# How many maxima scores each group takes, by weights of two engines' work, and the order of heads in the exp scores

## The chip, the cores and the metric

The kernel runs on one core of one Trainium2 chip. The metric is the device time of one execution in microseconds; the times shown are medians of a few executions.

## The reference, cut to what matters

The input has 8 batches of 1024 tokens of width 256. A block of attention with 16 query heads and 4 key heads of width 16, and then a linear layer with weights of -1, 0 and 1, each between two layer norms and with a residual:

```python
h = layernorm(x)                                  # over the 256 columns
q, k, v = h @ Wq, h @ Wk, h @ Wv                  # 256, 64, 64 columns
q, k = rope(q), rope(k)                           # q over all 256 columns, k per head
scores = einsum('bhqd,bhkd->bhqk', q, k) / 16     # 16 heads, keys repeated 4 times
o = softmax(scores) @ v
x = x + layernorm(o @ Wo)
f = layernorm(x) @ (ternary(W) * alpha).T + bias
x = x + layernorm(f)
```

All is float32. The softmax subtracts the largest score of its row, so the largest score must be known before the exponentials are taken.

## The kernel before, in words

**Units, blocks, steps, scores.** A unit is half a batch, 512 queries; there are 16 units (`NU`). A unit has 4 blocks (`G`), a block 8 key tiles (`NK`), so there are 512 steps of one key tile each (`NSTEP`), and a step has four matmuls of exp scores. The index `s` counts exp scores, from 0 to 2047; 128 of them make a unit, 32 a block.

**Two passes over the scores.** Each score is made twice on TensorE. `max_scores(v)` (line 582) makes 128 queries by 512 keys in one half of a PSUM tile `sm` of two banks; VectorE reduces the tile to row maxima `mx` (line 607), in one instruction of 1024 elements, or in two of 512 where `reduce_early` takes the first half at the end of a group. There are 2048 such scores too, two to a tile, and two `sm` buffers. When a block's maxima are complete, `shift_join`, `shift_rows` (a transpose `pm`, line 630) and `shift_low` (`ml`, on VectorE) split the maxima into a high and a low part, and a DMA writes them into spare rows of the queries `q_st`, so that the second matmul subtracts them by itself. `exp_one(s)` (line 655 for the matmul `se`, line 671 for the exponential `e` on ScalarE) makes 128 keys by 512 queries of one head group. Its tiles `se` come from a pool of three PSUM banks, which the other stages share: every transpose and product (`pt_xt`, `pt_ot`, `pq`, `pkv`, `pa`, `pf`, `pm`) takes one of the three. `e` has 12 buffers.

**Row halves.** The four heads of a step are two in rows 0 to 63 of the array and two in rows 64 to 127 (`a` is 0 or 1). Maxima scores have a half as well: from the second block on, two maxima of one tile are on one half, and the next tile's on the other. In PE's queue an exp score and a maxima score follow each other, and the two can be in the array together if their halves differ.

**Groups.** `window(s)` issues a group: `window_size(s)` exp scores, two or three, interleaved with maxima scores; then stages of other work that are ready (`do_parts`); then the products with the values, `av_piece` (line 691), of the group two groups back. From score 40 on (`REGULAR`) a group has two exp scores when a stage that needs a PSUM bank is ready, and that one stage; else three exp scores and none. The tensor engine's order is written by hand in this way (`tc.manual_schedule`), VectorE's and ScalarE's too; GpSimd's is left to the scheduler in the middle part.

**How far the maxima are ahead.** `maxima_by(s)` is the number of maxima scores that must have been issued when exp score `s` is: `s + 40`, and 2 more at six points, so `s + 52` from score 100 on. Before, a group takes as many maxima as bring the count to it: apart from the six points as many as it has exp scores. The last 13 steps have no maxima left, and `exp_two` makes their scores in `sm` tiles.

**Other stages.** `todo` maps a step to stages: `P_PARTS` for the projections of a later unit (`begin` is a layer norm's statistics on VectorE, `x` transposes, `kv_and_dram`, `q`, `v`), `T_PARTS` for what follows attention in the unit before (`invert` is a reciprocal on VectorE, `attn` the product with `Wo`, `stats_a`, `stats_x`, `stats_f` are statistics on VectorE, `ffn` the linear layer). The pattern recurs every 128 exp scores.

Of the kernel before, what the change touches and what calls it, by code (L numbers as in the profile page):

```python
# [28 lines left out]
def kernel(  # L29
# [35 lines left out]
    NK = S // P  # L65
# [4 lines left out]
    NSTEP = NU * SPU  # L70
    LEAD, START = 13, 10
# [121 lines left out]
    ffn = {}  # L193
# [361 lines left out]
    def block_queries(i, r2=slice(None)):  # L555

        u, j = divmod(i, G)
        if u < NU - 1:
            return q_st[u % 2][:, j, r2, :]
        return q_st[u % 2][:, :, r2, j * P : (j + 1) * P]  # L560

    def head_and_tile(i, r2, t):
        return r2 * UT + t if i // G < NU - 1 else 2 * t + r2

    def max_scores(v):


        i, k = divmod(v // 2, 2 * NK)
        u, part = i // G, v % 2
        if i == 0:  # L570
            a, ch, t, r2 = 1 - part, k // NK, k // 2 % UT, k % 2
        else:
            a, ch, t, r2 = 1 - k % 2, part, k // 4, k // 2 % 2
        queries = block_queries(i, r2)
        queries = queries[:, t * P : (t + 1) * P] if u < NU - 1 else queries[:, t]
        if part == 0:
            sm[0] = ps_mx.tile([P, 2, 512], F32, tag="sm", name=f"sm_{i}_{k}")
            if k == 0:
                mx[i] = small.tile([P, 2, 2 * UT, 2], F32, tag="mx", name=f"mx_{i}")
            reduced.clear()  # L580
        rows = slice(64 * a, 64 * a + 64)
        scores = nc.tensor.matmul(  # L582
            sm[0][:, part, :],
            queries[rows],
            k_st[(u // UPB) % 3][rows, r2, ch * 512 : (ch + 1) * 512],
            start=True,
            stop=True,
        )
        if part == 0:
            return  # L590
        if reduced:
            tc.declare_no_dep(scores.ins, early[0], reason="another bank")
        if i == 0:
            nc.vector.tensor_reduce(
                mx[i][:, ::-1, head_and_tile(i, r2, t), ch], sm[0], AX.X, ALU.max
            )
        else:
            reduce_halves(i, k, 2)
        if k == 2 * NK - 1:
            shift_join(i)  # L600
            due.append((v // 4 + (1 if i < 3 else 2), i))

    def reduce_halves(i, k, n):

        lo = len(reduced)
        a, t, r2 = 1 - k % 2, k // 4, k // 2 % 2
        early[0] = nc.vector.tensor_reduce(  # L607
            mx[i][:, a, head_and_tile(i, r2, t), lo:n], sm[0][:, lo:n, :], AX.X, ALU.max
        ).ins
        reduced.extend(range(lo, n))  # L610

    def reduce_early(v):

        i, k = divmod(v // 2, 2 * NK)
        if i > 0 and v % 2:
            reduce_halves(i, k, 1)
# [3 lines left out]
    def shift_join(i):  # L620

        m = mhl[i] = small.tile([P, 2, 2, 2 * UT], F32, tag="mc", name=f"mc_{i}")
        halves = mx.pop(i).unsqueeze(2).to_broadcast([P, 2, 2, 2 * UT, 2])
        nc.vector.tensor_reduce(m, halves, AX.X, ALU.max)
# [26 lines left out]
    def exp_scores(n, r2, a, sc):  # L651
        i, kt = divmod(n, NK)
        queries = block_queries(i, r2)
        rows = slice(64 * a, 64 * a + 64)
        nc.tensor.matmul(  # L655
            sc if len(queries.shape) == 2 else sc.rearrange("p (j t) -> p j t", j=G),
            k_st[(i // G // UPB) % 3][rows, r2, kt * P : (kt + 1) * P],
            queries[rows],
            start=True,
            stop=True,  # L660
        )

    def exp_one(s):

        n, (a, r2) = s // 4, divmod(s % 4, 2)
        assert n // NK in shifts
        i, kt = divmod(n, NK)
        e = es[n, r2, a] = ep.tile([P, UQ], F32, tag="e", name=f"e_{i}_{kt}_{r2}_{a}")
        sc = ps_e.tile([P, 512], F32, tag="se", name=f"se_{i}_{kt}_{r2}_{a}")
        exp_scores(n, r2, a, sc)  # L670
        nc.scalar.activation(e, sc, AF.Exp, scale=1.0 / D**0.5)  # L671

    def exp_two(n, r2):

        i, kt = divmod(n, NK)
        sc = ps_mx.tile([P, 2, 512], F32, tag="sm", name=f"se_{i}_{kt}_{r2}")
        for a in range(2):
            exp_scores(n, r2, a, sc[:, a, :])
        for a in range(2):
            e = es[n, r2, a] = ep.tile([P, UQ], F32, tag="e", name=f"e_{i}_{kt}_{r2}_{a}")  # L680
            nc.scalar.activation(e, sc[:, a, :], AF.Exp, scale=1.0 / D**0.5)

    def av_piece(i, first, end):

        va = v_aug[(i // G // UPB) % 3]
        if first == 0:
            av_ps[0] = ps_av.tile([P, UQ], F32, tag="av", name=f"av_{i}")
        for kt in range(first // UQ, (end - 1) // UQ + 1):
            lo, hi = max(first - kt * UQ, 0), min(end - kt * UQ, UQ)
            for r in (1, 2, 3, 0):  # L690
                nc.tensor.matmul(  # L691
                    av_ps[0][32 * r : 32 * r + 32, lo:hi],
                    va[:, kt, r, :],
                    es[i * NK + kt, r // 2, r % 2][:, lo:hi],
                    start=(kt == 0 and lo == 0),
                    stop=(kt == NK - 1 and hi == UQ),
                )
# [341 lines left out]
    def maxima_by(s):  # L1039

        return s + 4 * START + 2 * sum(s >= k for k in (28, 36, 52, 68, 84, 100))

    def banked(f, args):

        return f in (shift_rows, threshold, transpose_ternary) or (
            f is part and args[2] in ("x", "q", "v", "kv_and_dram", "attn", "ffn", "n", "o")
        )

    REGULAR = 40
    ends = 4 * (NSTEP - LEAD)  # L1050


    ready = []

    def window_size(s):


        left = 4 * NK - s % (4 * NK)
        if s >= ends:
            return 4  # L1060
        if s == 6:
            return 2
        size = min(2 if s >= REGULAR and any(banked(*p) for p in ready) else 3, left, ends - s)
        if left - size == 1:
            size += 1 if size == 2 else -1
        return size

    maxima = [0]

    def collect(n):  # L1070

        if due and due[0][0] <= maxima_by(4 * n + 4) // 4 - 1:
            i = due.pop(0)[1]
            ready.insert(0, (shift_rows, (i,)))
        ready.extend(todo.pop(n, ()))

    def do_parts(banks):

        while ready:
            f, args = ready[0]  # L1080
            if banked(f, args):
                if banks == 0:
                    break
                banks -= 1
            ready.pop(0)
            f(*args)
            if f is shift_rows:
                split_later.append(args[0])

    def take_low():  # L1090
        while split_later:
            shift_low(split_later.pop(0))

    def start_step(n):
        for q in range(4):
            max_scores(maxima[0])
            maxima[0] += 1
            if q == 1:
                take_low()
        collect(n)  # L1100
        do_parts(99)
# [3 lines left out]
    def av_windows(lag):  # L1105

        while len(behind) > lag:
            i, s, size = behind.pop(0)
            first = s % (4 * NK)
            av_piece(i, first * P, (first + size) * P)  # L1110
            if first + size == 4 * NK:
                done.append(i)

    def window(s):


        late, size = s >= ends, window_size(s)
        if done:
            av_out(done.pop())
        if late:  # L1120
            for r2 in range(2):
                exp_two(s // 4, r2)
        else:
            end = min(maxima_by(s + size), 4 * NSTEP)
            for q in range(max(size, end - maxima[0])):
                if q < size:
                    exp_one(s + q)
                if maxima[0] < end:
                    max_scores(maxima[0])
                    maxima[0] += 1  # L1130
                if q == 0:
                    take_low()
            reduce_early(maxima[0])
        take_low()
        behind.append((s // (4 * NK), s, size))
        for n in range(s // 4, (s + size) // 4):
            collect(n)
        do_parts(3 - size if REGULAR <= s < ends else 99)
        av_windows(1 if late else 2)
        return s + size  # L1140

    E = mybir.EngineType
    due, picks = [], []
    with tc.manual_schedule(engines={E.PE, E.DVE, E.Activation, E.Pool}):
# [52 lines left out]
        s = 0  # L1197
        while s < 8:
            s = window(s)
    with tc.manual_schedule(engines={E.PE, E.DVE, E.Activation}):  # L1200
        while s < 4 * NSTEP:
            s = window(s)
# [73 lines left out]
```

## Time and profile before

| | us |
|---|---|
| median of 3 runs | 1642.32 (1642.08 to 1643.09) |
| the profiled execution | 1642.63 |
| its span, first to last instruction | 1640.8 |
| PE, DVE, ACT, POOL busy | 1579.7, 1399.3, 1274.8, 835.4 |
| first exp score at | 62.7 |
| one unit of 128 exp scores, in the middle | about 96.4 |

The first 62.7 us are the start; from there to about 1620 us the pattern of groups runs; the rest is the last unit's tail. PE is TensorE's matmuls, PEld its weight loads (each matmul has one), DVE is VectorE and ACT is ScalarE. [...] Ends of matmuls are modelled.

### The profile page before, as it was taken

What the parts mean: (1) busy time and instruction counts of PE and PEld (TensorE: products, weight loads), DVE (VectorE), ACT (ScalarE), POOL (GpSimd) and SP (SyncE); (2) the same over time, 40 slices, a digit from 0 to 9 for tenths busy, and PEclk for the clock granted to TensorE, in tenths of its full rate; (3) what the DMA queues carried; (4) which work ended last, traced back from release to release, by engine and by line L of the source; (5) the groups of instructions that cost most, each with busy time, mean ns of one, the idle gap of its engine ahead of it and who ended that gap; (6) DMA issues with size and microseconds to landing.
All of it is one profiled execution on the core that took longest, in us unless ns stands there. A gap on an engine that the chain in (4) does not pass through costs nothing.

```text
span 1640.8 us, 37250 instructions
## 1 busy us (share of the span) xinstructions
PE 1579.7 (96%) x14712; PEld 818.5 (50%) x14712; DVE 1399.3 (85%) x2049; ACT 1274.8 (78%) x2479; POOL 835.4 (51%) x1239
## 2 busy tenths in 40 slices
PE   7999999999999999999999999999999999999997
PEld 5544455454545545454544545455454544444544
DVE  7778788889898888989889898988989888898964
ACT  4657778878787887878788787887878787877884
POOL 5532457374653737455373835547374552323363
PEclk8989999999999999999999999999999999999999
DMA  4151425125151422515133251513325151231100
GB/s 139 53 101 34 91 77 101 59 76 101 56 106 49 91 67 82 101 46 105 60 83 75 77 106 44 104 49 89 71 67 104 40 97 42 46 70 34 42 15 27
DMA packets 86079, 117.99 MB, mean 72 GB/s; under 512 B 12088, under 2 KB 50808, under 8 KB 85752
## 3 DMA queue, kind: packets, MB, share of 16 engines
q1 hardware_dynamic: 85904, 115.60, 29.9%
q8 instruction: 116, 1.90, 0.5%
q14 instruction: 59, 0.48, 0.1%
HBM read 68.65 MB, written 45.88 MB: 70 GB/s over the span
## 4 chain that ended last, share of the span: by engine, by line
PE 80%; DVE 10%; DMA 3%; ACT 2%; POOL 2%; issue 2%; SPq 1%; POOLq 0%; DVEq 0%; ACTq 0%
PE av L691 28%; PE se L655 28%; PE sm L582 9%; DVE mx L607 7%; PE pa L283 3%; PE pq L283 2%; PE pf L283 2%; PE pt_ot L267 2%; ACT e L671 2%; PE pt_xt L267 2%; PE pkv L283 2%; DMA q_st<-ml 1%; DMA k_rot<-d_k 1%; PE pm L630 1%; DMA dk<-ks 1%
## 5 line engine op out<-in xcount | busy, mean ns | idle before, releaser
L607 DVE TENSOR_REDUCE mx<-sm 128x2 f32<-128x1024 f32 (+1 forms) x1304 | 1205.3, 973 | 191.9 <-PE sm L582 174.1
L671 ACT ACTIVATE e<-se 128x512 f32<-128x512 f32 x1996 | 1058.2, 602 | 223.0 <-PE sm L582 172.4
L582 PE MATMUL sm<-k_st,q_st 64*128 64x512 f32 x2048 | 748.4, 450 | 6.9 <-DVE mx L607 3.9
L655 PE MATMUL se<-q_st,k_st 64*128 64x512 f32 x2048 | 705.5, 441 | 26.7 <-ACT e L671 14.4
L691 PE MATMUL av<-e,v_aug 128*32 128x256 f32 (+3 forms) x8608 | 607.2, 378 | 0.0
L655 PEld LDWEIGHTS se<-q_st,k_st 64*128 64x128 f32 x2048 | 324.9, 185 | 405.7 <-ACT e L671 302.1
L582 PEld LDWEIGHTS sm<-k_st,q_st 64*128 64x128 f32 x2048 | 326.1, 185 | 65.1 <-DVE mx L607 41.9
L691 PEld LDWEIGHTS av<-e,v_aug 128*32 128x32 f32 x8608 | 194.4, 108 | 211.0 <-issue 148.3
L241 POOL TENSOR_SCALAR lnsc<-mv 128x2 f32<-128x2 f32 (+1 forms) x134 | 25.8, 193 | 400.1 <-DVE mv L239 395.1
L765 POOL TENSOR_TENSOR xn<-xn,a 128x512 f32<-128x512 f32 x30 | 38.4, 1282 | 131.8 <-DMA a<-d_rec 101.2
L826 POOL TENSOR_TENSOR a<-a,bias_bc 128x512 f32<-128x512 f32 x30 | 38.6, 1287 | 108.3 <-ACT a L825 108.3
L242 POOL TENSOR_TENSOR lnsc<-lnsc,mhalf 128x2 f32<-128x2 f32 (+1 forms) x134 | 92.5, 691 | 0.9
L162 POOL TENSOR_TENSOR hl<-xn,hl 128x512 fp32r<-128x512 f32 x60 | 76.5, 1287 | 0.4
L253 POOL TENSOR_SCALAR xn<-x,lnsc 128x256 f32<-128x256 f32 x116 | 65.1, 570 | 2.2
L237 DVE BATCH_NORM_STATS2 bnst<-a 128x6 f32<-128x256 f32 x120 | 44.5, 413 | 4.6 <-POOL a L826 4.6
L297 POOL TENSOR_TENSOR t<-q_rot,sin_q_sb 128x512 f32<-128x512 f32 x31 | 39.9, 1288 | 15.5 <-ACT q_rot L439 15.4
L283 PE MATMUL pa<-woh,hl 128*128 128x256 f32 x240 | 46.2, 294 | 1.1 <-ACT e L671 1.1
L283 PE MATMUL pq<-xt,wqkvh 128*128 128x256 f32 x256 | 45.8, 303 | 0.5 <-ACT e L671 0.5
L237 DVE BATCH_NORM_STATS2 bnst<-x 128x6 f32<-128x256 f32 x124 | 45.9, 412 | 0.4 <-DMA x<-in_L_attn_x 0.4
L271 ACT CAST ot<-pt_ot 128x512 fp32r<-128x512 f32 x66 | 39.6, 601 | 4.7 <-PE pt_ot L267 4.7
L439 ACT COPY q_rot<-pq 128x512 f32<-128x512 f32 x32 | 18.8, 586 | 30.9 <-PE pq L283 30.9
L162 POOL TENSOR_TENSOR hlq<-q_rot,hlq 128x512 fp32r<-128x512 f32 x31 | 39.8, 1285 | 4.8 <-ACT hlq L159 4.5
(157 smaller groups left out, 1303.1 us busy)
## 6 DMA issues: line engine op xcount, KB each, us to landing
q_st<-dq SPq DMA_DIRECT2D x90, 256.0 KB
dq<-hlq SPq DMA_DIRECT2D x60, 256.0 KB
d_av<-avsb SPq DMA_DIRECT2D x60, 256.0 KB
x<-in_L_attn_x SPq DMA_DIRECT2D x15, 512.0 KB
xn<-d_av SPq DMA_DIRECT2D x30, 256.0 KB
a<-d_rec SPq DMA_DIRECT2D x30, 256.0 KB
xr<-in_L_attn_x SPq DMA_DIRECT2D x15, 512.0 KB
out_x<-a SPq DMA_DIRECT2D x30, 256.0 KB
```

The costliest lines, as they stand in the source:

```text
L162: eng.tensor_tensor(lo, src, hi.bitcast(F32), ALU.subtract)
L237: nc.vector.bn_stats(st[:, t, :], src[:, t, :])
L242: nc.gpsimd.tensor_tensor(sc[:, 1, :], sc[:, 1, :], mhalf[:, :n], ALU.pow)
L253: eng.tensor_scalar(dst[:, t, :], src[:, t, :], sc[:, 0, t : t + 1] if eng is nc.gpsimd else mv[:, t, 0:1], sc[:, 1, t : t + 1], ALU.add i ...
L267: nc.tensor.transpose(pt[:, c, t * P : (t + 1) * P], src[:, t, c * P : (c + 1) * P], ident_r)
L283: nc.tensor.matmul(out, chunk(left[i], c), chunk(right[j], c), start=(k == 0), stop=(k == len(steps) - 1),)
L297: eng.tensor_tensor(dst, x, table.unsqueeze(1).to_broadcast(list(x.shape)), ALU.mult)
L582: scores = nc.tensor.matmul(sm[0][:, part, :], queries[rows], k_st[(u // UPB) % 3][rows, r2, ch * 512 : (ch + 1) * 512], start=True, stop= ...
L607: early[0] = nc.vector.tensor_reduce(mx[i][:, a, head_and_tile(i, r2, t), lo:n], sm[0][:, lo:n, :], AX.X, ALU.max).ins
L655: nc.tensor.matmul(sc if len(queries.shape) == 2 else sc.rearrange("p (j t) -> p j t", j=G), k_st[(i // G // UPB) % 3][rows, r2, kt * P : ...
L671: nc.scalar.activation(e, sc, AF.Exp, scale=1.0 / D**0.5)
L691: nc.tensor.matmul(av_ps[0][32 * r : 32 * r + 32, lo:hi], va[:, kt, r, :], es[i * NK + kt, r // 2, r % 2][:, lo:hi], start=(kt == 0 and lo ...
```

## The change

A group no longer takes a fixed number of maxima. `maxima_of(s, size)` keeps an account `behind_by` of how far VectorE's work is behind TensorE's, in units of about 10 ns. For each possible number `n` (1, 3 or 5 in a group of three; 2 or 4 in a group of two; never below what `maxima_by` asks, and never over 12 ahead of it) it reckons the tensor engine's time and VectorE's, and takes the largest `n` that leaves the account under 60. Stages enter with weights of their own (`W_PE`, `W_DVE`). Below score 40 the number is what it was.

`pairs(size, n)` writes the order in the group: two maxima of different halves may follow each other, and an exp score ahead of a maxima score is taken from the other half. So the exp scores of a block no longer come in the order of `s`: `waiting` has a list for each half, and `exp_next(a)` takes the next of one. A block's shift falls due by the number of maxima issued (5 or 9 after its last), and it is asked for in every group rather than at whole steps. The end of the maxima is found by counting (`ended`) rather than fixed at 13 steps.

```diff
-            due.append((v // 4 + (1 if i < 3 else 2), i))
+            due.append((v + (5 if i < 3 else 9), i))
...
-    def exp_one(s):
-        n, (a, r2) = s // 4, divmod(s % 4, 2)
+    waiting = [[], []]
+    def exp_next(a):
+        n, r2 = waiting[a].pop(0)
...
     REGULAR = 40
-    ends = 4 * (NSTEP - LEAD)
+    AHEAD = 12
...
+    def ended(s):
+        return maxima[0] == 4 * NSTEP and s % 4 == 0 and len(waiting[0]) == len(waiting[1])
...
+    W_SCORES, W_PAIR, W_AV, W_AV_COLS, W_MAX = 19, 23, 14, 21, 58
+    W_PE = {"q": 162, "attn": 162, "kv_and_dram": 162, "ffn": 113, "v": 33}
+    W_DVE = {"begin": 92, "stats_a": 92, "stats_x": 92, "stats_f": 92, "invert": 46}
+    place = [0]
+    behind_by = [60]
+    def part_weight(table, f, args, default):
+        return table.get(args[2], default) if f is part else default
+    def maxima_of(s, size):
+        least = min(maxima_by(s + size), 4 * NSTEP) - maxima[0]
+        if s < REGULAR or maxima[0] == 4 * NSTEP:
+            return max(least, 0)
+        other = [part_weight(W_PE, *p, 44) for p in ready if banked(*p)][: 3 - size]
+        best = None
+        for n in range(2 - size % 2, 6, 2):
+            if n < least or maxima[0] + n > min(maxima_by(s + size) + AHEAD, 4 * NSTEP):
+                continue
+            time = W_SCORES + W_PAIR * (n + size) // 2 + W_AV + W_AV_COLS * size + sum(other)
+            rest = behind_by[0] + W_MAX * n - time
+            if best is None or rest < SLACK:
+                best = n
+        return max(least, 0) if best is None else best
+    SLACK = 60
+    def sm_half(v):
+        i, k = divmod(v // 2, 2 * NK)
+        return 1 - v % 2 if i == 0 else 1 - k % 2
+    def pairs(size, n):
+        first = maxima[0]
+        halves = [sm_half(first + k) for k in range(n)]
+        left = [len(w) for w in waiting]
+        def exp_on(a):
+            a = a if left[a] else 1 - a
+            left[a] -= 1
+            return a
+        order, k = [], 0
+        while k < n:
+            if size < n - k and k + 1 < n and halves[k] != halves[k + 1]:
+                order += ["max", "max"]
+                k += 2
+            elif size:
+                order += [exp_on(1 - halves[k]), "max"]
+                size -= 1
+                k += 1
+            else:
+                order.append("max")
+                k += 1
+        for _ in range(size):
+            order.append(exp_on(0 if left[0] >= left[1] else 1))
+        return order
...
     def do_parts(banks):
+        if due and due[0][0] <= max(maxima[0], maxima_by(place[0])):
+            ready.insert(0, (shift_rows, (due.pop(0)[1],)))
         while ready:
             f, args = ready[0]
             if banked(f, args):
                 if banks == 0:
                     break
                 banks -= 1
+                behind_by[0] -= part_weight(W_PE, f, args, 44)
+            behind_by[0] += part_weight(W_DVE, f, args, 0)
...
     def window(s):
...
-            end = min(maxima_by(s + size), 4 * NSTEP)
-            for q in range(max(size, end - maxima[0])):
-                if q < size:
-                    exp_one(s + q)
-                if maxima[0] < end:
+            n = maxima_of(s, size)
+            order = pairs(size, n)
+            behind_by[0] += W_MAX * n - W_SCORES - W_PAIR * len(order) // 2
+            for q, what in enumerate(order):
+                if what == "max":
                     max_scores(maxima[0])
                     maxima[0] += 1
-                if q == 0:
+                else:
+                    exp_next(what)
+                if q == 1:
                     take_low()
...
+        behind_by[0] = max(0, behind_by[0] - W_AV - W_AV_COLS * size)
```

More of the change, by code (lines that the diff above doesn't have):

```diff
@@ L1049 @@
     REGULAR = 40
-    ends = 4 * (NSTEP - LEAD)
+    AHEAD = 12
     ready = []
+    def ended(s):
+        return maxima[0] == 4 * NSTEP and s % 4 == 0 and len(waiting[0]) == len(waiting[1])
     def window_size(s):
         left = 4 * NK - s % (4 * NK)
-        if s >= ends:
-            return 4
         if s == 6:
             return 2
-        size = min(2 if s >= REGULAR and any(banked(*p) for p in ready) else 3, left, ends - s)
+        size = min(2 if s >= REGULAR and any(banked(*p) for p in ready) else 3, left)
+        if maxima[0] == 4 * NSTEP:
+            size = min(size, 4 - s % 4)
         if left - size == 1:
@@ L1068 @@
     maxima = [0]
     def collect(n):
-        if due and due[0][0] <= maxima_by(4 * n + 4) // 4 - 1:
-            i = due.pop(0)[1]
-            ready.insert(0, (shift_rows, (i,)))
         ready.extend(todo.pop(n, ()))
     def do_parts(banks):
+        if due and due[0][0] <= max(maxima[0], maxima_by(place[0])):
+            ready.insert(0, (shift_rows, (due.pop(0)[1],)))
         while ready:
@@ L1114, in window @@
     def window(s):
-        late, size = s >= ends, window_size(s)
+        late = ended(s)
+        place[0] = s
+        size = 4 if late else window_size(s)
+        if s % (4 * NK) == 0:
+            for n in range(s // 4, s // 4 + NK):
+                for a in range(2):
+                    waiting[a] += [(n, r2) for r2 in range(2)]
         if done:
@@ L1122, in window @@
                 exp_two(s // 4, r2)
-        else:
-            end = min(maxima_by(s + size), 4 * NSTEP)
-            for q in range(max(size, end - maxima[0])):
-                if q < size:
-                    exp_one(s + q)
-                if maxima[0] < end:
+            for w in waiting:
+                del w[:2]
+        else:
+            n = maxima_of(s, size)
[3 more added lines that the diff above has]
+                if what == "max":
                     max_scores(maxima[0])
                     maxima[0] += 1
-                if q == 0:
+                else:
+                    exp_next(what)
+                if q == 1:
                     take_low()
@@ L1137, in window @@
             collect(n)
-        do_parts(3 - size if REGULAR <= s < ends else 99)
+        do_parts(3 - size if s >= REGULAR and not late else 99)
         av_windows(1 if late else 2)
+        behind_by[0] = max(0, behind_by[0] - W_AV - W_AV_COLS * size)
         return s + size
```

## The prediction

> **What bounds the kernel now.** I read the page's chain first, then the waits, then VectorE by form, then one unit of 128 exp scores as stretches and in order of time.
>
> ```profile
> PE 80%; DVE 10%; DMA 3%; ACT 2%; POOL 2%; issue 2%; SPq 1%; POOLq 0%; DVEq 0%; ACTq 0%
> ```
> The tensor engine's queue carries the chain; VectorE has a tenth of it, 0.10 x 1640.8 = 164 us. The waits, as engine and line, releaser, total us, times, longest:
>
> ```profile
> PEld se L655 <- ACT e L671: 302.1, 651, 0.9
> DVE mx L607 <- PE sm L582: 174.1, 274, 3.4
> PEld sm L582 <- DVE mx L607: 41.9, 127, 1.4
> ```
> These are weight loads; the long first row is partly covered by matmuls still running. The third row is what VectorE's lateness leaves idle at the loads, the second what VectorE waits for scores: it is late in some groups and idle in others. By form (busy us, mean ns):
>
> ```profile
> L607 DVE TENSOR_REDUCE mx<-sm 128x2 f32<-128x1024 f32 x712 | 855.3, 1216 | 167.5 <-PE sm L582 153.2 <-PE se L655 11.0
> L607 DVE TENSOR_REDUCE mx<-sm 128x1 f32<-128x512 f32 x592 | 381.9, 680 | 24.5 <-PE sm L582 20.9
> ```
> In the timeline the starts of two in a row are 1.13 us apart for the first form (803.00 and 804.13) and 0.60 for the second. A group of three takes one of each, 1.73 us; the fastest group of three takes 1.46 us from first exp score to next (838.38 to 839.85). So VectorE falls behind in runs of such groups and catches up where a product stands in the group. One unit, in three stretches (length; PE, PEld, DVE, ACT, POOL busy):
>
> ```profile
> 774.94:788.00 13.06, 12.61 (x124) 5.55 (x120) 12.95 (x20) 10.69 (x22) 4.90 (x8) 1.00 0.34 110
> 788.00:806.24 18.24, 18.22 (x177) 9.87 (x173) 15.08 (x20) 14.30 (x28) 5.38 (x6) 1.00 0.03 9
> 806.24:855.81 49.57, 48.29 (x467) 25.84 (x463) 41.89 (x62) 39.00 (x76) 34.99 (x52) 1.00 0.27 76
> ```
> VectorE is full in the first (12.95 of 13.06), has 3.2 us left in the second and 7.7 in the third. Why it is full: a layer norm's statistics and a reciprocal among the maxima.
>
> ```profile
> 775.38 0.74 DVE L237 BATCH_NORM_STATS2 bnst<-x 128x6 f32<-128x256 f32 x2
> 776.03 0.30 DVE L239 BATCH_NORM_AGGREGATE mv<-bnst 128x2 f32<-128x6 f32 x2
> 776.26 0.33 DVE L639 SCALAR_TENSOR_TENSOR ml<-mh,low,pm 32x128 fp32r<-32x128 f32 x1
> ...
> 781.12 0.53 DVE L752 RECIPROCAL den<-den 128x64 f32<-128x64 f32 x1
> ```
> What it costs the tensor engine: in a pair both loads should start together, and here the third is split.
>
> ```profile
> 780.56 0.19 PEld L655 LDWEIGHTS se<-q_st,k_st 64*128 64x128 f32 x1
> 780.57 0.19 PEld L582 LDWEIGHTS sm<-k_st,q_st 64*128 64x128 f32 x1
> 780.80 0.18 PEld L655 LDWEIGHTS se<-q_st,k_st 64*128 64x128 f32 x1
> 781.24 0.18 PEld L582 LDWEIGHTS sm<-k_st,q_st 64*128 64x128 f32 x1 [0.26 <-DVE mx L607]
> ```
> The products behind it wait too: this group lasts 780.46 to 782.46, 2.00 us.
>
> **What the Trainium skill says.** "TensorEngine Tiling (Array Packing)", Key Properties: different tiles of the array load weights and multiply in parallel. The trace agrees: loads of opposite halves start within 0.01 us (780.56, 780.57). Where the halves are equal, as at 118.68 to 120.37, the four matmuls start at 118.68, 119.02, 119.25 and 119.49, so a score alone takes about 0.23 us. "TensorE: Matmul & The Clock Gate", Part 3, The mechanism: matmuls keep their order, start and end; so a late maxima score holds all behind it, as above. "VectorE: DVE Perf Modes", The perf-mode tier table: `tensor_reduce` has only the 1x mode; no faster form is behind 1216 and 680 ns. "Perfetto Trace Analysis", Identifying the Most-Contended Engine: matmul occupancy is no measure of headroom; 96% here goes with the waits listed.
>
> **The change, part by part.** From the built order: 793 groups in both. 64 groups of three exp scores take one maxima score instead of three, and 66 groups of two with a stage take four instead of two; about 380 of some 450 plain groups of three stay as they are. Reductions: 728 full and 592 half before, 712 and 624 after: 32 x 0.60 - 16 x 1.13 = +1 us of VectorE. In the middle the pattern recurs per unit: four of the first kind and four of the second.
>
> *(a) Relief.* Two of the four light groups stand at scores 920 and 928, right behind the statistics and the reciprocal, in the first stretch. They take 2 x 1.13 = 2.26 us of maxima out of it. The splits between an exp load and its maxima load there (0.33 at 777.45, 0.44 at 780.80, 0.21 at 782.57, 0.48 at 784.62, 0.23 at 786.42, 0.28 at 788.48) sum to 2.0 us; I take 1.9 off the path. What is late next is the exponential: three take 1.46 us at their 0.485 us spacing, so the light group doesn't go below that.
>
> *(b) Where they go.* The other two light groups (947 and 957) and the four heavy ones (945, 950, 952, 960) lie in the second stretch: net four maxima more, 2.3 us of reductions in 3.2 us of room. On PE a heavy group has a third slot: 4 x 0.23 = +0.92. A light group saves a slot only if its two last exp scores differ in half; in the built order 33 of 64 have equal halves, so about 2 x 0.23 = -0.46. The four maxima need both `sm` tiles within some 0.3 us, and the stage's product stands behind them in PE's queue, as do its evacuation and the next exp scores: I add 0.35 for tiles not yet free. Sum +0.8.
>
> *(c) Shifts.* `pm` at 918 shares a group with `begin`, and the group after it takes 2.40 us (774.94 to 777.34) instead of 1.68. After the change the shift comes 13 exp scores earlier and apart from it. Of four shifts per unit, two had a group of three behind them, after it one: -0.3. The two DMAs of a shift (8 KB each) and those of `stack_queries` keep their order on SP; the maxima of a unit start up to 12 scores, 12 x 0.75 = 9 us, earlier, which leaves 60 scores, 45 us, from the issue of its queries' load at score 128(u-1)+4, so I cost that at nothing; without this cover it would be a wait of its landing at each unit. `xr` and the projections' loads don't move.
>
> *(d) The order of heads.* Exp scores of a half may now run ahead, so the products with the values meet a younger `e`: in four groups per unit the youngest `e` that a first product needs has only one exp score behind it, against three groups in the whole kernel before. No wait of that size is in the trace (PEld av on ACT e is 5.1 us in 21). Bounds: nothing, where the stage between covers it; 0.7 us each at most (exponential of the second score of a group ends 1.6 us after its start, the products begin at 0.9). I take 0.1 each, +0.4, keeping 0 to 2.8.
>
> Per unit -1.9 + 0.8 - 0.3 + 0.4 = -1.0 us, in ten units (3 to 12): -10. In units 13 to 15 the loads' idle time for VectorE is larger (5.0 us in 1339 to 1432 against 1.6 in the unit shown), and there are about five light groups each, most behind statistics: -2.5 + 1.2 + 0.3 = -1 each, -3. Between scores 40 and 100 the count ahead was not a multiple of four for about 48 scores, so exp and maxima scores were of equal halves; they now differ: 24 pairs or so x 0.23 = 5.5, part under other waits, -4. The start (62.7 us) and the tail keep their work; the maxima end up to 12 scores sooner, which frees VectorE where nothing waits for it: 0. Sum -17 against the profiled execution (1642.63, 1.8 more than its span and 0.3 over the median): 1626 us.
>
> **The rivals.** *More than that:* all of VectorE's share of the chain is in play; if a third of its 164 us goes, 1590 to 1608. For it: it idles 174 us waiting for scores. Against it: the 302 us of waits for exponentials, unchanged, and most groups keep their number. 0.12. *No effect:* the wait for VectorE turns into one for the exponential; (a) falls to 0.6 and the sum to between -8 and +3. For it: 1.46 us of exponentials in a group of 1.68. 0.20. *Slower, by the order of heads:* the products in av wait for a young `e`, at 4 places per unit; at 0.35 us each a unit's sum is nought, from 0.5 each on the whole is over 0.2% slower, and at 0.7 a unit loses 1.4 us: 13 units +18, less 4: 1646 to 1657. For it: PE keeps its order, so the wait is paid in full. Against it: the next exp scores wait for ScalarE anyhow. 0.16. *That it does not do what it says* is excluded for the order, which shows the numbers above; what is open is whether weights in steps of 10 ns follow the true backlog. The forecast has 0.52.
>
> **How the numbers follow.** A measurement of this kernel can tell about 0.2%, 3.3 us. Faster: 0.52 + 0.12 + half of the no-effect case, 0.10 = 0.74; same 0.09; slower 0.16 + 0.01 = 0.17. The forecast's own range is 1615 to 1634, from (d) at 0, (a) at 2.0 and (b) without its 0.35 (-5, -1, -5) up to (d) at 0.2 each and no gain in units 13 to 15 (+5, +3). For 8 in 10 it reaches to 1604 and 1647, into both outer cases.
>
> **What would show it.** Right: 0.3 us or less between the loads of a pair behind `begin` and `invert`; PEld sm waiting for DVE mx under 30 us; DVE's share of the chain down to 5 to 7%; a middle unit in about 95.4 us. (d) shows as a row of av waiting for e, over 20 us if the slow rival holds. Wrong: units of 96 us or more, or a gain that lies before score 100 alone.

## The result, and the profile after

The changed kernel takes 1667.2 us (1666.98 to 1668.79); the kernel before took 1642.24 beside it. The ratio is 1.0153, 95% interval 1.0135 to 1.0171: 25 us slower where 16 us faster was forecast. The profiled execution took 1666.98 us with a span of 1665.2, against 1642.63 and 1640.8.

The page's chain and the row of the tensor engine, of the changed kernel:

```profile
PE 1607.2 (97%) x14736; PEld 829.9 (50%) x14736; DVE 1402.9 (84%) x2065; ACT 1275.0 (77%) x2479; POOL 834.9 (50%) x1239
...
PE 75%; DVE 13%; DMA 5%; POOL 4%; ACT 2%; issue 2%; SPq 1%; POOLq 0%; ACTq 0%
```
VectorE's share of the chain rose from 10 to 13% where it was to fall, and PE's busy time grew by 27.5 us with the same number of score matmuls. The waits of the changed kernel:

```profile
PEld se L655 <- ACT e L673: 244.4, 588, 0.9
DVE mx L607 <- PE sm L582: 179.5, 273, 5.7
...
ACT e L673 <- PE se L655: 63.3, 113, 4.9
PEld sm L582 <- DVE mx L607: 53.8, 125, 1.2
...
PEld av L693 <- ACT e L673: 12.8, 58, 0.4
```
The wait of a maxima score for VectorE, which the change was to shorten, grew from 41.9 to 53.8 us. ScalarE waits twice as long for exp scores (31.8 before), which fits a heavy group (two exp scores, four maxima), where two or three maxima stand ahead of an exp score. The loads' wait for exponentials fell by 58 us, and the kernel is slower all the same.

The same three stretches of one unit (exp scores 920 to 940, 940 to 962, 962 to 1024), in the changed kernel:

```profile
792.91:805.22 12.31, 12.27 (x120) 5.43 (x116) 11.15 (x18) 10.92 (x22) 4.05 (x7) 1.00 0.40 126
805.22:825.47 20.25, 19.95 (x189) 10.96 (x186) 16.59 (x20) 14.42 (x28) 6.17 (x6) 1.00 0.04 15
825.47:874.16 48.69, 48.52 (x459) 25.63 (x456) 42.18 (x65) 38.76 (x76) 34.96 (x52) 1.00 0.28 77
```
The relieved stretch is 0.75 us shorter, the one with the heavy groups 2.01 us longer, the third 0.88 shorter; exp scores 896 to 920, ahead of them, take 0.72 more (16.59 against 15.87). A unit is 1.1 us longer: the ten units from score 384 on take 96.2 to 97.3 us in the kernel before, 96.7 on average, and 97.8 to 97.9 in the changed one. In the stretch that grew, VectorE did 1.5 us more and still idled 3.7.

Where the whole 24.4 us arose, in the profiled executions, from the starts of exp scores 128, 384 and 1664 in the timelines (us). The rows e1 to e12 are the experiments described below:

| kernel | to 128 | 128-384 | 384-1664 | to the end |
|---|---|---|---|---|
| before | 177.0 | 195.5 | 966.9 | 301.4 |
| changed | 179.0 | 205.8 | 978.5 | 301.9 |
| e1, counts as before | 179.3 | 196.3 | 967.1 | 303.1 |
| e2, heads in order | 180.5 | 211.5 | 981.3 | 313.3 |
| e5, light groups opposite | 180.3 | 205.0 | 971.2 | 303.2 |
| e6, heavy beside long products | 177.1 | 205.4 | 976.2 | 299.9 |
| e7, before with 12 of lead | 176.6 | 208.7 | 969.7 | 298.5 |
| e8, stage groups one more | 176.8 | 202.6 | 990.9 | 304.4 |
| e9, plain groups one more | 176.0 | 206.0 | 1002.3 | 310.8 |
| e10, e5 and e6 together | 177.8 | 204.5 | 974.6 | 300.2 |
| e11, e10 with 4 ahead | 180.6 | 199.5 | 974.8 | 299.5 |
| e3, before, half reductions | 170.0 | 193.3 | 939.3 | 282.6 |
| e4, changed, half reductions | 163.2 | 197.9 | 954.9 | 288.3 |
| e12, e3 with 12 of lead | 167.6 | 201.1 | 934.1 | 283.1 |

Two places stand out: ten units in the middle, 11.6 us, and the two units in which the maxima gain their lead (their count ahead of the exp scores goes from 52 to 64), 10.3 us. Each row is one execution. The programs of before, e7, e8 and e9 are alike up to score 128 and differ there by 1.1 us; those of e3 and e12 differ by 2.4, so small differences in the first column are not read. Ratios below are medians against the kernel before run beside them, and expectations in us are best compared by the ratio, since that kernel's own median lay between 1642 and 1646 us.

### The profile page after: what moved, and what is told of

It is laid out like the page before. It is cut to its first block, busy times and chain, and to the rows that moved or that the text cites. A ratio compares the mean times of both kernels' runs of the same rounds, so it can differ in the third digit from the quotient of the medians.

```text
span 1665.2 us, 37317 instructions
## 1 busy us (share of the span) xinstructions
PE 1607.2 (97%) x14736; PEld 829.9 (50%) x14736; DVE 1402.9 (84%) x2065; ACT 1275.0 (77%) x2479; POOL 834.9 (50%) x1239
## 4 chain that ended last, share of the span: by engine, by line
PE 75%; DVE 13%; DMA 5%; POOL 4%; ACT 2%; issue 2%; SPq 1%; POOLq 0%; ACTq 0%
PE av L693 27%; PE se L655 24%; PE sm L582 10%; DVE mx L607 10%; PE pa L283 3%; PE pq L283 2%; PE pt_ot L267 2%; PE pkv L283 1%; ACT e L673 1%; PE pf L283 1%; PE pt_xt L267 1%; DMA q_st<-fill_d 1%; PE pm L630 1%; DMA d_av<-avsb 1%; DVE bnst L237 1%
## 5 line engine op out<-in xcount | busy, mean ns | idle before, releaser
L607 DVE TENSOR_REDUCE mx<-sm 128x1 f32<-128x512 f32 (+1 forms) x1320 | 1209.5, 964 | 208.1 <-PE sm L582 179.5
L582 PE MATMUL sm<-k_st,q_st 64*128 64x512 f32 x2048 | 733.2, 451 | 13.2 <-DVE mx L607 6.7
L655 PE MATMUL se<-q_st,k_st 64*128 64x512 f32 x2048 | 708.7, 440 | 13.2 <-DMA q_st<-ml 9.3
L693 PE MATMUL av<-e,v_aug 128*32 128x256 f32 (+2 forms) x8632 | 621.3, 378 | 0.3
L582 PEld LDWEIGHTS sm<-k_st,q_st 64*128 64x128 f32 x2048 | 320.8, 186 | 87.2 <-DVE mx L607 53.8
L693 PEld LDWEIGHTS av<-e,v_aug 128*32 128x32 f32 x8632 | 201.1, 108 | 217.7 <-issue 145.6
L271 ACT CAST xt<-pt_xt 128x512 fp32r<-128x512 f32 x64 | 37.3, 590 | 15.6 <-PE pt_xt L267 15.5
```

The lines of the kernel that those rows point to most:

```text
L271: copy(dst, pt.bitcast(F32))
L582: scores = nc.tensor.matmul(sm[0][:, part, :], queries[rows], k_st[(u // UPB) % 3][rows, r2, ch * 512 : (ch + 1) * 512], start=True, stop= ...
L607: early[0] = nc.vector.tensor_reduce(mx[i][:, a, head_and_tile(i, r2, t), lo:n], sm[0][:, lo:n, :], AX.X, ALU.max).ins
L655: nc.tensor.matmul(sc if len(queries.shape) == 2 else sc.rearrange("p (j t) -> p j t", j=G), k_st[(i // G // UPB) % 3][rows, r2, kt * P : ...
L693: nc.tensor.matmul(av_ps[0][32 * r : 32 * r + 32, lo:hi], va[:, kt, r, :], es[i * NK + kt, r // 2, r % 2][:, lo:hi], start=(kt == 0 and lo ...
```

## The experiments

**Is it the counts? e1.**

```diff
-        if s < REGULAR or maxima[0] == 4 * NSTEP:
-            return max(least, 0)
+        return max(least, 0)
```


> The changed kernel, but each group takes the number of maxima that maxima_by asks for, as before; the order of heads by row halves and the earlier shifts stay. Theory 'counts': the heavy groups (two exp scores, four maxima, a stage) lost the time; then about 1642, 1636 to 1648. Theory 'order of heads': the younger e in front of the value products lost it; then 1655 or more. Theory 'shifts': the earlier transposes pm lost it; then 1655 or more too.

Measured: ratio to the kernel before 1.0003 (0.9992 to 1.0014). All of the loss goes with the counts, and with them the lead; what else is new, the order by halves below score 100 and the due rule, moves nothing that can be told.

**Is it the order of heads? e2.**

```diff
     def exp_next(a):
+        a = min((w[0][0], k) for k, w in enumerate(waiting) if w)[1]
         n, r2 = waiting[a].pop(0)
```


> The changed kernel with its numbers of maxima and its shifts, but the exp scores of a block come in the order of s again, so that pairs of equal halves occur after light and heavy groups. Theory 'order of heads': the loss goes, 1640 to 1650. Theory 'counts': the loss stays or grows by the pairs that no longer overlap (0.23 us each), 1662 to 1690. Theory 'shifts': 1662 or more.

Measured: 1687.8 us, ratio 1.0255 (1.0234 to 1.0275), some 17 us over the changed kernel's ratio. With these counts the order by halves is needed: after a light group the two sequences are shifted by two, and in order the pairs have equal halves up to the next such group: behind the one at 920 none of the next 6 maxima scores starts within 0.1 us of an exp score, where 5 do in the changed kernel. The order costs something itself: from the kernel before to the changed one the row of av waiting for e grew from 5.1 to 12.8 us, well below the loss.

**Is it waiting for VectorE? e3 and e4.** In both kernels, and in the same way in the first block's reduction:

```diff
-mx[i][:, a, head_and_tile(i, r2, t), lo:n], sm[0][:, lo:n, :], AX.X, ALU.max
+mx[i][:, a, head_and_tile(i, r2, t), lo:n], sm[0][:, lo:n, :256], AX.X, ALU.max
```


> The kernel before, with each row maximum taken over the first 256 of 512 columns: the other half of the keys is left out of the maxima, so VectorE has some 0.27 us less per maxima score and is no limit. It prices what VectorE costs the kernel before. The prediction put that at some 2 to 3.5 us per unit for late maxima: 1590 to 1615. If the wait turns into one for the exponential, 1625 to 1640.

> The changed kernel with the same cut in the maxima (the first 256 of 512 columns). Theory 'counts, by waiting for VectorE' (the four maxima of a heavy group wait for an sm tile that VectorE still reads): with VectorE quick the two kernels come together, under 8 us above the kernel before with the same cut. Theory 'counts, by slots of the tensor engine' or 'order of heads': the 25 us between the two stay, 18 us or more.

Measured: 1588.7 us (0.9662, 0.9643 to 0.9682) and 1607.4 us (0.9781, 0.9756 to 0.9806). VectorE does cost the kernel before 55 us (1.0 less 0.9662, of 1642.2); that part of the reading was right. But between the two kernels 0.0119 stay, 19.5 us of the 25 (14 to 25 by the intervals), although the wait of a maxima load for VectorE is down to 3.3 us in e3 and 11.8 in e4. In the middle units (exp scores 384 to 1664), of e3:

```profile
363.30:1302.60 939.30, 920.33 (x9164) 469.83 (x9160) 546.63 (x1227) 777.19 (x1521) 530.98 (x773) 1.00 0.34 79
```
and of e4:

```profile
361.10:1316.00 954.90, 947.39 (x9246) 485.51 (x9242) 547.54 (x1247) 775.94 (x1521) 530.34 (x773) 1.00 0.34 78
```
VectorE is busy 547 us of 939 and of 955: no limit in either. PE is busy 27 us more in the second. Without VectorE as a limit the new counts cost 15.6 us here; with it they cost 11.6. So the relief is worth some 4 us in ten units, 0.4 each: an estimate, since it is a difference between four executions and the units of e3 range from 93.4 to 94.7 us. Most of the price does not come from a late VectorE. The second stretch (scores 940 to 962) shows it, of e3:

```profile
766.52:784.26 17.74, 17.74 (x177) 9.52 (x173) 9.21 (x20) 14.08 (x28) 5.46 (x8) 1.00 0.02 6
```
and of e4:

```profile
771.09:790.66 19.57, 19.52 (x189) 10.82 (x185) 10.36 (x23) 14.19 (x28) 5.32 (x7) 1.00 0.03 10
```
It grows by 1.83 us where VectorE is quick, against 2.01 us where it is not.

**What is a slot worth? e8 and e9.** The kernel before, with one maxima matmul made twice in some groups:

```diff
+        if part == 0 and twice[0]:
+            twice[0] = False
+            nc.tensor.matmul(sm[0][:, part, :], queries[rows],
+                k_st[(u // UPB) % 3][rows, r2, ch * 512 : (ch + 1) * 512], start=True, stop=True)
...
+            twice[0] = s >= 128 and size == 2 and any(f is part and args[2] in ("x", "attn") for f, args in ready)   # e8
+            twice[0] = s >= 128 and size == 3   # e9
```


> The kernel before, with one maxima matmul made twice (the same values into the same place) in each group of two exp scores that has a transposing stage x or the product attn: 160 matmuls more, no more work for VectorE or ScalarE. Theory 'slots': such groups are bound by the tensor engine, so 160 x 0.23 = 37 us more, 1673 to 1682. Theory 'held by the exponentials or by VectorE': under 15 us more.

> The kernel before, with one maxima matmul made twice in each group of three exp scores from unit 1 on: 424 matmuls more, no other work. If plain groups are bound by the tensor engine: 424 x 0.23 = 98 us more. If they are held by the exponentials and VectorE, so that a slot taken out of them brings nothing either: under 50 us more, some 0.1 each. The theory that light groups give nothing back asks for clearly less per matmul here than in the stage groups.

Measured: 1.0187 (1.0164 to 1.0211) and 1.0325 (1.0303 to 1.0346), of 1642.2 us: 31 us for 160 matmuls, 0.19 each (0.17 to 0.22), and 53 us for 424, 0.126 each (0.117 to 0.134). Of the 0.23 us of a slot, most is paid in a group with a stage and little over half in a plain one. The expectation put the second under 50 us; it is a little over, and the order of the two is as the theory asks. So by these prices a pair that is moved from a plain group to a stage group costs about 0.07 us even when the plain group gives its slot up in full.

**Do light groups give it up? e5.**

```diff
-        for _ in range(size):
-            order.append(exp_on(0 if left[0] >= left[1] else 1))
+        for k in range(size):
+            order.append(exp_on(1 - order[-1] if k else 0 if left[0] >= left[1] else 1))
```


> The changed kernel; in a light group (three exp scores, one maxima score) the last two exp scores are taken from opposite halves, so that 63 of the 64 light groups have two slots on the tensor engine, against 29 before. Theory 'slots' (light groups don't give back the slot that heavy ones take, because of equal halves): 34 x 0.23 = 8 us less than the changed kernel, about 1659. Theory 'held by the exponentials' (a light group waits for ScalarE or for the value products whatever its slots): no change, 1664 to 1670. Theory 'order of heads': a few us either way by the age of e.

Measured: 1659.6 us, 1.0091 (1.0073 to 1.0109). Against the changed kernel's 1.0153 that is 10 us less (6 to 14), where the theory of slots asked for 8. In the middle units 978.5 becomes 971.2, and every unit there takes 97.1 or 97.2 us. So of 11.6 us there, 7.3 go with light groups whose last two exp scores had one half. In the changed kernel's timeline such a group, from 811.61 on:

```profile
811.61 0.49 PE L655 MATMUL se<-q_st,k_st 64*128 64x512 f32 x1
811.62 0.50 PE L582 MATMUL sm<-k_st,q_st 64*128 64x512 f32 x1
811.95 0.62 PE L655 MATMUL se<-q_st,k_st 64*128 64x512 f32 x2
812.51 1.19 PE L693 MATMUL av<-e,v_aug 128*32 128x256 f32 x16
```
The two exp scores of the third row take 0.62 us together and not 0.39: they are in a row, and the next group starts at 813.62. In e5 the same group lasts 1.53 us instead of 2.01. About half of that is the slot; the products `av` behind it take 0.94 us there and not 1.19, in which their loads wait 0.20 us for an exponential. So e5 takes away a slot and, here, a wait for a young `e` too.

**Are heavy groups beside transposes the dear ones? e6 and, with e5, e10.**

```diff
         for n in range(2 - size % 2, 6, 2):
+            if size == 2 and n > 2 and sum(other) < 100:
+                continue
```


> The changed kernel, but four maxima only in groups whose stage is a long product (attn, q, kv_and_dram, ffn), not beside transposes: 36 heavy and 35 light groups instead of 68 and 64. Theory 'each heavy group costs its slot and its wait': 32 heavy groups less, of 0.5 to 0.7 us each, and the light ones gave nothing: 1645 to 1652. Theory 'the exchange is neutral and something else lost the time': 1662 or more.

> The two repairs together: four maxima only beside long products, and opposite halves at the end of light groups (36 heavy and 35 light groups). If slots, transposing stages and the lead add up: the changed kernel less 8 (half of the light groups are left, so 4 of them) less 8: 1652 to 1656, and what is left over the kernel before is the lead. If weights can win at all with these counts: under 1642.

Measured: 1659.5 us (1.0090, 1.0072 to 1.0108) and 1657.9 us (1.0073, 1.0053 to 1.0093). By the ratios e6 is 10 us below the changed kernel (6 to 14), where 15 to 22 were expected, and e10 is 12 us over the kernel before, within the 10 to 14 expected. Whether the two repairs add up, the intervals do not tell. In the middle units half of the heavy groups less brought only 2.3 us, and the restricted kernel with opposite halves is 3.4 us slower there than e5. So the heavy groups beside transposes are not dearer than the rest in sum, long as they look. The trace of e6 shows where the gain went: the two heavy groups that a unit keeps, at 950 and 960, last 3.60 and 3.94 us there instead of 3.10 and 3.35, and in each a maxima load now waits for VectorE, 0.47 and 0.58 us.

**What does the lead cost? e7, e11 and e12.** The kernel before with more lead; the restricted kernel with `AHEAD = 4`; and e3 with more lead.

```diff
-        return s + 4 * START + 2 * sum(s >= k for k in (28, 36, 52, 68, 84, 100))
+        return s + 4 * START + 2 * sum(s >= k for k in (28, 36, 52, 68, 84, 100, 184, 200, 216, 232, 248, 264))
```


> The kernel before with its fixed counts, except that the maxima gain 12 more scores of lead, two at each of six points between scores 184 and 264; the shifts then come 12 scores earlier as in the changed kernel. Theory 'the lead is paid for': the 12 scores cost 12 x 0.57 = 7 us of VectorE where VectorE is short, and come back only at the end, where it is not: 1646 to 1652, the rise between scores 180 and 280, and units alike from there on. Theory 'the lead is free': 1640 to 1644. If the earlier shifts matter, units after score 384 differ from before by over 0.2 us each.

> As the run before, with at most 4 maxima ahead of maxima_by instead of 12 (27 heavy and 26 light groups). Theory 'the lead is paid for': 8 scores less, 3 to 5 us less than the run before, 1647 to 1652. Otherwise the same time as the run before, or more, since the weights have less room.

> The kernel before with 12 more scores of lead, gained between scores 184 and 264, and with each row maximum over the first 256 of 512 columns (half of the keys is left out of the maxima). Beside the run of the kernel before with the same cut (1588.7 us, 193.3 us from exp score 128 to 384) it prices the lead where VectorE is no limit. If the 13 us that the lead took in this stretch are VectorE's, at most 12 x 0.23 = 3 us are left: 193 to 197 us in the stretch, 1587 to 1593 in all. If they are the order of heads and halves, the slots or the earlier shifts: 202 us or more, 1597 or more.

Measured: e7 1.0061 (1.0041 to 1.0081), 10 us: 13.2 us more between exp scores 128 and 384, 2.8 more in the ten units after, 3 less at the end. In that stretch, of the kernel before:

```profile
177.04:372.54 195.50, 189.43 (x1836) 97.28 (x1832) 169.16 (x240) 156.44 (x305) 107.35 (x153) 1.00 0.36 84
```
and of e7:

```profile
176.60:385.30 208.70, 200.88 (x1864) 103.86 (x1860) 176.78 (x250) 157.08 (x305) 107.37 (x153) 0.99 0.34 79
```
VectorE's and PE's work grow by 7.6 and 11.5 us while VectorE was already busy 87% of the time. But e7 changes more than the lead. After every other of its six points the count ahead is no multiple of four for 16 exp scores, and then an exp score and its maxima score have equal halves. A group of e7 in such a stretch:

```profile
281.54 0.51 PE L655 MATMUL se<-q_st,k_st 64*128 64x512 f32 x2
281.88 0.41 PE L582 MATMUL sm<-k_st,q_st 64*128 64x512 f32 x2
282.13 0.39 PE L655 MATMUL se<-q_st,k_st 64*128 64x512 f32 x1
282.36 0.39 PE L582 MATMUL sm<-k_st,q_st 64*128 64x512 f32 x1
```
In the three stretches (184 to 200, 216 to 232, 248 to 264) 5 of 55 maxima scores start within 0.1 us of an exp score; in the kernel before it is 41 of 46. Of the 13.2 us, 9.7 lie in these three. e12, the same lead where VectorE is no limit, has the same fault: its stretch grows by 7.8 us (201.1 against 193.3), and 6.6 of them lie in the three. So e7 and e12 price the lead together with equal halves and cannot tell them apart. In all e12 is at 0.9689 against e3's 0.9662, intervals overlapping (0.9673 to 0.9705 and 0.9643 to 0.9682).

Two other pairs keep the halves opposite. In this stretch e11 gains 4 scores of lead and e10 10, and e11 takes 5.0 us less, 0.8 per score; in that are 6 heavy and 3 light groups fewer. In the whole kernel the two, 1.0054 (1.0033 to 1.0075) and 1.0073, are not apart. And from e3 to e4, which both have VectorE quick, the stretch grows by 4.6 us instead of 10.3. So the lead is not free, and more than half of what this stretch loses goes when VectorE is quick; how the rest divides into slots and earlier shifts stays open.

No version of the exchange that was tried beat the kernel before.

## Why the prediction was wrong, point by point

**(a) Relief: the direction right, the size wrong, and the gain not where it was looked for.** Predicted -1.9 us in the first stretch; measured -0.75. Nearly all of that is one group, at 920, which lasts 1.69 us instead of 2.40. The largest wait in it, in the kernel before, was not for VectorE:

```profile
776.12 0.18 PEld L655 LDWEIGHTS se<-q_st,k_st 64*128 64x128 f32 x1 [0.88 <-ACT e L671]
```
With VectorE quick, in e3, this group still lasts 2.41 us. The light group at 928 goes from 2.00 to 1.68 us, and that is taken back by the groups at 926 (1.44 to 1.68) and at 934 (2.30 to 2.42), the latter with a late load that had been taken off too. So the mis-sized term is the sum of late loads taken off the path: 1.9 us, of which the light groups brought about nothing here beyond the group at 920. The floor of 1.46 us was not it: in e5, with opposite halves, the group at 928 lasts 1.45.

**(b) Where they go: the step that failed in the middle.** Predicted +0.8 for the second stretch; measured +2.0. The lengths of its groups, averaged over the ten middle units, split the sum (us per unit; the last column has VectorE quick):

| part | predicted | changed less before | e4 less e3 |
|---|---|---|---|
| third slot of four heavy groups | +0.92 | +0.98 | +0.93 |
| wait for a tile in a heavy group | +0.35 | +0.85 | +0.55 |
| scores of all other groups | -0.46 | -0.15 | +0.02 |
| products `av` | in (d) | +0.34 | +0.34 |

The slots were priced rightly; with the 0.19 and 0.126 us of e8 and e9 their sum, four taken and two given back, would be nearly the same, +0.5 for +0.46. Two terms were mis-sized. The first is what the light groups give back. The one at 947 saves no slot for its equal halves, and the products behind it wait besides; with opposite halves, in e5, the stretch is 0.5 us shorter. The one at 957 is quicker by 0.6 us, but the plain group in front of it is slower by as much (1.46 to 2.03), and with VectorE quick neither changes. The second is the wait for a tile, 0.85 us and not 0.35, and all of it in one group. The loads of a heavy group in the changed kernel:

```profile
809.08 0.19 PEld L582 LDWEIGHTS sm<-k_st,q_st 64*128 64x128 f32 x1
809.31 0.18 PEld L655 LDWEIGHTS se<-q_st,k_st 64*128 64x128 f32 x1
810.16 0.18 PEld L582 LDWEIGHTS sm<-k_st,q_st 64*128 64x128 f32 x1 [0.67 <-DVE mx L607]
810.58 0.39 PEld L267 LDWEIGHTS pt_xt<-ident_r,xs 128*128 128x128 f32 x4 [0.24 <-POOL hl L162]
```
The fourth maxima score starts 0.85 us after its exp score, and the transpose behind it waits with it. The Trainium skill has the rule, in "TensorE: Matmul & The Clock Gate", Part 3, The mechanism: matmuls keep their order; here the transpose starts at 810.59, behind the late score at 810.16. The prediction applied it to the heavy groups too, at too low a price. That VectorE has 3.2 us of room in a stretch does not mean that it is free at the moment when two tiles are asked for; even at half the length its reductions hold this group for 0.55 us.

**The lead: a term that the sum did not have.** "Up to 12 ahead" was followed only to the queries' load, and costed at nothing there. The 12 scores have to be made once in addition, in units where VectorE is short, and come back at the end where nothing waits for them. Between scores 128 and 384, where the changed kernel has 13 heavy groups and 7 light ones, that stretch grows by 10.3 us. Two units of the exchange as in the middle would be 2.3 of them, so the lead is left with some 8 us, an estimate. The 5.0 us for 6 scores of e10 against e11 are of that size. In the prediction's own prices it was 12 x 0.57 = 7 us; it was not asked who pays.

**(c) Shifts.** Predicted -0.3 per unit. e7 moves the shifts by as much, with plain counts, and its middle units are 0.28 us longer each on average (97.0, against 96.2 to 97.3), not shorter. With VectorE out of the way they take 93.4 us each (e12), which is what the quickest units of e3 take too (93.4 to 94.7). A gain from the shifts is not shown.

**(d) The order of heads.** Predicted +0.4 per unit with 0 to 2.8 as bounds; the wait of av for e rose by 7.7 us at the loads in the whole kernel, half a microsecond per unit. Right in size as far as these waits tell, and the slower rival, which rested on it, accounts by them for 7.7 us of the 25 at most.

**Below score 100.** Predicted -4 for pairs that no longer have equal halves. e1 has them: between scores 40 and 100, 53 of 68 maxima scores start within 0.1 us of an exp score, against 22 of 64 in the kernel before. It gains nothing by it: 49.5 us against 48.7. What holds these groups instead was not followed.

**The rivals.** The mechanism of the slower case was the wrong one. What held is in steps (a) and (b): -1.0 us per unit was a difference of -2.2 and +1.2, and an error of 40% in two terms turns it round. The range did not take that in, and left the lead out altogether.

## What to carry to other kernels

A move of work between two places has two prices, and the price in each place is measured by adding one instruction there: here 0.19 us against 0.126 for the same matmul. Count the gain only when the place that is relieved is shown to give its time up: here it was held by something else, an exponential or two scores on one half of the array. And the place that receives has to be free at the moment, not on average, since all that stands behind in an in-order queue waits with it. What a wait for an engine costs can be tested by making that engine quick, as e3 and e4 do. Whatever lets one pass run further ahead has to be built up once: ask in which stage that is paid and whether the stage that gets it back was waiting. When such a lead is priced by an experiment, see that it changes nothing else; e7 and e12 changed the halves as well.

## What was not expected of the hardware

In the changed kernel the first shift falls due at once, so its transpose waits at the head of PE's queue:

```profile
55.22 0.37 PE L630 MATMUL pm<-ident,mc 128*32 128x128 f32 x1 [2.10 <-DVE mc L624]
55.25 0.81 PE L267 MATMUL pt_xt<-ident_r,xs 128*128 128x128 f32 x4
...
66.89 0.79 PE L655 MATMUL se<-q_st,k_st 64*128 64x512 f32 x1
```
After 2.10 us of idling (and 0.45 shortly before) four transposes take 0.81 us instead of 0.53, and a first exp score is shown with 0.79 us instead of 0.47, until about 74 us. The granted clock is 0.50 in every five microseconds from 55 to 70 us, though PE is busy for nearly all of them. The row of the granted clock shows it in the second slice; of the kernel before:

```profile
PEclk8989999999999999999999999999999999999999
```
and of the changed kernel:

```profile
PEclk8799999999999999999999999999999999999999
```
The kernel before has such a stretch as well, only shorter and later, around a wait of 2.73 us for a DMA:

```profile
62.70 0.47 PE L655 MATMUL se<-q_st,k_st 64*128 64x512 f32 x1 [2.73 <-DMA q_st<-ml]
```
Its granted clock is 0.84 from 60 to 65 us, 0.50 from 65 to 70 and 0.97 after. In e4 the same transpose waits less, and the clock stays at 1.00 from 45 to 80 us:

```profile
52.49 0.27 PE L630 MATMUL pm<-ident,mc 128*32 128x128 f32 x1 [1.51 <-DVE mc L624]
52.51 0.53 PE L267 MATMUL pt_xt<-ident_r,xs 128*128 128x128 f32 x4
```
Counted from the pair of maxima scores ahead of the stall (52.62 us here, 52.36 before), the first exp score starts 3.9 us later than in the kernel before. In the six other runs with this stall, e1, e2, e5, e6, e10 and e11, it is 2.8 to 3.5. Of the changed kernel's delay 0.8 us are left at score 40 and 2.0 at score 128, which is within what runs of one program differ by there. What gave it back was not followed.
